# Reciprocal roots by GpSimd's power, and a router's logits and largest eight computed batch by batch in the attention ahead of it

## The chip, the cores and the metric

The kernel runs on one core of a Trainium2 chip. The core has five engines with an instruction stream each: TensorE (PE, with its weight loads PEld), VectorE (DVE), ScalarE (ACT), GpSimd (POOL) and SyncE (SP), which here only issues DMAs. They work side by side and wait for each other through semaphores. The metric is the device time of one execution in microseconds (us); the value compared is the median over runs.

## The reference

A decoder of four layers works on x, 8 sequences of 256 tokens of 256 numbers (2048 tokens). Each layer has three parts, and each part is followed by a residual sum and a layer norm:

```python
def _layernorm(x, axis=-1, eps=1e-05):
    m = jnp.mean(x, axis=axis, keepdims=True)
    v = jnp.var(x, axis=axis, keepdims=True)
    return (x - m) / jnp.sqrt(v + eps)
...
x = _layernorm(x + _L1_xattn_ref(x, ctx_768, ...), axis=-1)
x = _layernorm(x + _L1_ffn_ref(x, ...), axis=-1)
```

The parts that the change touches are five attentions (l0_attn, l0_xattn, l1_attn, l1_xattn, l2_attn; an "xattn" attends to a context of 120 tokens), l3_ffn, a feed-forward in fixed point, and l1_ffn, a mixture of 32 experts of which each token takes 4:

```python
logits = x @ gate_w.T                        # 2048 x 32
probs = jax.nn.softmax(logits, axis=-1)
topk_w, topk_idx = jax.lax.top_k(probs, K)   # K = 4
topk_w = topk_w / jnp.sum(topk_w, axis=-1, keepdims=True)
e_flat = topk_idx.reshape(-1)
order = jnp.argsort(e_flat)
...
pos = jnp.arange(t * K) - starts[e_s]
slot = jnp.minimum(pos, C)                   # C = 256 places per expert
buf = jnp.zeros((E, C + 1, h), x.dtype).at[e_s, slot].set(x[t_s])
```

After it comes l2_xattn, which quantizes its weights to -1, 0 and 1 by the mean of their absolute values, one mean for each of seven matrices:

```python
w_scale = jnp.maximum(jnp.mean(jnp.abs(W)), 1e-05)
qW = jnp.sign(W) * (jnp.abs(W) > 0.5 * w_scale).astype(W.dtype)
```

## The kernel before

The whole state stays on the chip: `X` holds the 2048 tokens as 16 tiles of 128 tokens (tokens on the 128 partitions), `xT` the same transposed. A layer part is a method (`l0_attn`, `l1_xattn`, `l1_ffn`, ...), called in order by `build` (L1881); the weights of the next part are loaded, on SP's queue, into the other of two alternating weight tiles before a part begins. There is no order written out by hand: each engine's instructions are laid out by a scheduler from the program's order and the free buffers, and each engine then works through its own list strictly in order.

**The norm.** `finish_x` (L165) takes z, two tiles of 128x256. `norm_stats` (L141) computes mean and variance on DVE (L146, L147), and `rsqrt` (L126) turns the variance into 1/sqrt(v + eps) with DVE alone: an addition (L129), a first guess by integer arithmetic on the bits (L131), and three Newton steps of three instructions each (L134, L135, L137), all of them on tiles of 128x2. Then X = (z - mean) * rs_y (L170). `transpose_into_xT` (L150) transposes X on PE, and ACT copies it into `xT` (L157). There are 104 such calls of `rsqrt`, one for two tiles of 128 tokens each.

**The attentions of sixteen heads.** `attention16` (L571) runs l1_attn, l1_xattn and l2_attn over eight batches, software-pipelined: while the exponentials of batch b are made (`exps16`), the minima of batch b+1 (`low`, L445 and L461, in `largest16`) are reduced by DVE and the output projection of batch b-1 is done. `sums16` (L538) multiplies the exponentials with the values, divides (`sides` on ACT and DVE, L533 and L534, then `aT` on POOL, L536), adds the bias to X on POOL (`biased`, L558), projects, adds (z, L566) and finishes the norm. l0_attn has a loop of its own with the same end (`biased` L267, z L273). l0_xattn (L320) is a plain loop over batches: scores `psc`, their maximum `nm` (L352), exponential, transposition, product, z (L363), norm.

**The routing in l1_ffn** (L971). Once the norm of l1_xattn is complete, PE computes the logits of all 16 tiles (`plog`), and ACT copies them (L742). `route` (L737) takes the largest eight of each tile with their indices (L746, L747), makes one-hots `oh` in float32 (L753), their sum over the four choices `m` (L761), running sums over tiles `before` (L765), and with two matmuls per tile the position of each token in each expert's queue (`pos`). L1001 to L1009 turn positions into slots with a sentinel for full experts; `pick` (L774) selects each token's own slot with the one-hots (L779, L781); `place` (L1014) is the position inside the expert. `takers` (L797) inverts the map: for each tile and choice it compares `place` with the numbers 0 to 255 (`at`, L818, 64 of them) and multiplies this one-hot with `own`, which holds the token's numbers (L809, L810), so that `take` (L827) says which token stands in which place of which expert. X has been written to memory as `xd` on ACT's queue (L792). Each expert then gathers its 256 rows with two indirect DMAs of POOL (L834), transposes them (L849), multiplies with its weights `we` (loaded on SP's queue through three buffers) and writes its rows `y` to memory (`yd`). A shared expert (`ph` from `sgu`, `silu` L968, `shT` L969) is computed for all tokens ahead of the 32.

**The weights of l2_xattn** are prepared in the time of the experts: `ternary` (L1524) sums absolute values of the seven matrices on DVE (`w_sums`, L1534, from `l2x_flat`, 128 x 7680 numbers), POOL adds over the partitions (`w_scale`, L1538), and DVE compares (L1551, L1553). They lie in the tile of the next-but-one part, loaded while l1_xattn runs.

**l3_ffn** (`fixed_point`, L1438) works on 256 tokens at a time: two matmuls with large DVE passes over 128x2048 between them, z (L1481), norm. The last eight norms write the result.

Of the kernel before, what the change touches and what calls it, by code (L numbers as in the profile page):

```python
# [11 lines left out]
F32 = mybir.dt.float32  # L12
BF16 = mybir.dt.bfloat16
I32 = mybir.dt.int32
U32 = mybir.dt.uint32
AF = mybir.ActivationFunctionType
# [4 lines left out]
P = 128  # L21
# [21 lines left out]
class Net:  # L43
    def __init__(self, ctx: ExitStack, tc: tile.TileContext, ins, out):
# [41 lines left out]
        self.avg = self.const.tile([P, 2, B], F32, name="avg")  # L86
        self.w_scale = self.const.tile([P, len(L2X)], F32, name="w_scale")
        self.wset = 0

# [9 lines left out]

    def load(self, *specs, rows=(), flat=None):  # L100

        self.wset ^= 1
        srcs = [self.ins[name] for name, _ in specs]
        brow = [LAYOUT.rows[name] for name in rows]
        total = sum(src.shape[1] for src in srcs) + sum(n for _, n in brow)
        whole = self.wpool.tile([P, total], F32, name=f"w{self.wset}")
        out, o = [], 0
        for (name, kc), src in zip(specs, srcs):
            part = whole[:, o : o + src.shape[1]]
            self.nc.sync.dma_start(part, src)  # L110
            out.append(part.rearrange("p (c n) -> p c n", c=kc))
            o += src.shape[1]
        for at, n in brow:
            self.nc.sync.dma_start(whole[0:1, o : o + n], self.ins["rows"][:, at : at + n])
            out.append(whole[0:1, o : o + n])
            o += n
        return (out, whole) if flat else out

# [6 lines left out]

    def rsqrt(self, var, n):  # L126
        nc, tmp = self.nc, self.tmp
        v = tmp.tile([P, n], F32, name="rs_v")
        nc.vector.tensor_scalar(v, var, LN_EPS, None, ALU.add)  # L129
# [407 lines left out]

    def sums16(self, b, e, vps, sizes, wo, bo, work):  # L538

# [28 lines left out]

        return project_out, lambda: self.transpose_into_xT(2 * b, 1)

    def attention16(self, project, low, vps, sizes, causal, wo, bo, work):  # L571

# [15 lines left out]
        for b in range(B):  # L588
# [14 lines left out]
            values = vps[b // 2 % 2]  # L603
            before = self.sums16(b, e, [values[:, b % 2, t, :] for t in range(len(sizes))], sizes, wo, bo, work)
            if b % 2 == 0 and b + 2 < B:
# [34 lines left out]
    def load_l1_xattn(self):  # L640
        return self.load(*((f"l1x_w{n}", 2) for n in "qkvo"), rows=("l1x_bv", "l1x_bo"))

    def l1_xattn(self, w):
        nc = self.nc
        wq, wk, wv, wo, bv, bo = w
        with ExitStack() as ctx:
# [14 lines left out]

            self.attention16(project, low, vps, [SC], False, wo, bo, work)

# [301 lines left out]
    def silu_mul(self, out, pg, pu, shape, work):  # L965
# [3 lines left out]
        nc.vector.tensor_tensor(out, g, pu, ALU.mult)  # L969

    def l1_ffn(self, w):  # L971
        nc, tc = self.nc, self.tc
        gate = self.gate1
        E, K, C = 32, 4, 256
        DROP = E * C
        with (
# [10 lines left out]
            slot = keep.tile([P, NT, K], U32, name="slot")  # L987
            with tc.tile_pool(name="f1q", bufs=1) as pool:
                with tc.tile_pool(name="f1r", bufs=1, space=PSUM) as ps:
                    plog = ps.tile([P, NT, E], F32, name="plog")  # L990
                    for i in range(NT):
                        self.mm(plog[:, i, :], [(self.xT4[:, c, i, :], gate[:, c, :]) for c in range(2)])
                    m8, fi, oh, pos, _ = self.route(plog, E, K, pool, ps)
                    nc.vector.tensor_tensor(gw, m8[:, :, :K], m8[:, :, 0:1].to_broadcast([P, NT, K]), ALU.subtract)
                    nc.scalar.activation(gw, gw, AF.Exp)
                    total = pool.tile([P, NT], F32, name="total")
                    nc.vector.tensor_reduce(total, gw, AX.X, ALU.add)
                    nc.vector.reciprocal(total, total)
                    nc.vector.tensor_tensor(gw, gw, total.unsqueeze(2).to_broadcast([P, NT, K]), ALU.mult)
                    first = pool.tile([P, E], F32, name="first")  # L1000
                    nc.vector.tensor_scalar(first, self.cst("iota")[:, :E], float(C), None, ALU.mult)  # L1001
                    full = pool.tile([P, NT, E], F32, name="full")
                    nc.vector.tensor_single_scalar(full, pos, float(C), ALU.is_ge)
                    slotf = pool.tile([P, NT, E], F32, name="slotf")
                    nc.vector.tensor_tensor(slotf, pos, first.unsqueeze(1).to_broadcast([P, NT, E]), ALU.add)
                    left = pool.tile([P, NT, E], F32, name="left")
                    nc.vector.tensor_scalar(left, slotf, -1.0, float(DROP), ALU.mult, ALU.add)
                    nc.vector.tensor_tensor(left, left, full, ALU.mult)
                    nc.vector.tensor_tensor(slotf, slotf, left, ALU.add)  # L1009
                xd = self.in_dram(pool, dram)  # L1010
                slot4 = self.pick(oh, slotf, K, E, pool, "slot4")
                nc.vector.tensor_copy(slot, slot4)
                place = pool.tile([P, NT, K], F32, name="place")
                nc.vector.scalar_tensor_tensor(place, fi, -float(C), slot4, ALU.mult, ALU.add)  # L1014
                with tc.tile_pool(name="f1t", bufs=1, space=PSUM) as ps:
                    take = self.takers(place, oh, K, pool, work, ps, keep)
            pool = ctx.enter_context(tc.tile_pool(name="f1l", bufs=1))
# [133 lines left out]
    def l2_ffn(self, w):  # L1151
# [3 lines left out]
        with ExitStack() as ctx:  # L1155
# [23 lines left out]
            for _ in later:  # L1179
                pass  # L1180
            self.fixed_point(w4, pool, work, ps)

# [341 lines left out]
    def ternary(self, pool):  # L1524
# [4 lines left out]
        for name, k, n, count in L2X:  # L1529
            where[name] = (o, k // P, n, count)  # L1530
            o += k // P * n
        sums = pool.tile([P, len(L2X)], F32, name="w_sums")
        for j, (name, (o, kc, n, _)) in enumerate(where.items()):
            nc.vector.tensor_reduce(  # L1534
                sums[:, j : j + 1], w[:, o : o + kc * n], AX.X, ALU.add, apply_absolute_value=True
            )
        scale = self.w_scale
        nc.gpsimd.partition_all_reduce(scale, sums, P, bass_isa.ReduceOp.add)  # L1538
        for j, (_, _, _, count) in enumerate(where.values()):
# [338 lines left out]
LAYERS = [f"l{n}_{part}" for n in range(3) for part in ("attn", "xattn", "ffn")]  # L1878


def build(tc, ins, out, layers=LAYERS, tap=None):  # L1881
    with ExitStack() as ctx:
        net = Net(ctx, tc, ins, out)
        net.last = tap is None
        net.start()
        w = None
        for n, name in enumerate(layers):
            if w is None:
                w = getattr(net, f"load_{name}")()
            nxt = None  # L1890
            if n + 1 < len(layers):
                nxt = getattr(net, f"load_{layers[n + 1]}")()
            getattr(net, name)(w)
            w = nxt
        if tap:
            tap(net)
# [19 lines left out]
```

## Time and profile before

| | us |
|---|---|
| median of 3 runs | 2713.8 (2710.76 to 2717.37) |
| the profiled execution | 2858.3 |
| its span, first to last instruction | 2856.3 |
| mean granted clock of TensorE in it | 0.867 |

The profile is of a single execution, which took 144.5 us longer than the median; durations in the text below come from that execution. The stages, by their windows in it (us from the start of the span; busy us in the window):

| stage | window | PE | DVE | ACT | POOL | granted clock |
|---|---|---|---|---|---|---|
| l0_attn, last part | 170-216 | 46.0 | 32.8 | 4.4 | 8.3 | 0.74 |
| l0_xattn | 220-310 | 63.8 | 40.6 | 17.4 | 0.0 | 0.71 |
| l1_attn | 680-860 | 160.3 | 122.6 | 64.5 | 23.4 | 0.96 |
| l1_xattn | 860-1010 | 120.6 | 120.3 | 54.3 | 21.0 | 0.90 |
| l1_ffn, routing | 1013-1068 | 30.3 | 43.9 | 1.6 | 0.3 | 0.53 |
| l2_attn | 1250-1540 | 204.7 | 196.5 | 90.7 | 72.5 | 0.86 |
| l3_ffn | 2680-2856 | 140.2 | 148.8 | 61.9 | 0.0 | 0.90 |

What is not in the table: l0_ffn, with 8 experts (about 312 to 680), the 32 experts themselves (1092 to 1226), l2_xattn (1540 to 1700), and a long stretch in which l2_ffn, l3_attn and l3_xattn are interleaved (1700 to 2680).

How to read the lines in the prediction: a line of the timeline gives the start in us, the duration in us, the engine, the line of the kernel, the operation, output and inputs by the program's names, shape, how many instructions are merged in it, and in brackets how long the engine had been idle before it and what released it. A line of the costliest groups gives the count, then busy us and mean ns of one instruction, then the idle time of the engine before them and what ended it. A granted clock below 1 means that TensorE was held below full speed in that stretch.

### The profile page before, as it was taken

To read this page: it belongs to the slowest core of one execution; us is meant where nothing else is said; L and a number is where in the kernel's file an instruction comes from. 1 tells how busy PE (TensorE), PEld (TensorE's weight loads), DVE (VectorE), ACT (ScalarE), POOL (GpSimd) and SP (SyncE) were. 2 spreads that over 40 slices of the span, in tenths; PEclk is the share of its full clock that TensorE was granted. 3 is DMA by queue.
4 is the path that set the end of the run, shared out by engine and by line. 5 is a ranking of instruction groups with operands and counts; after the bars stand their busy time and mean duration, and the time that the engine had idled before them with its cause. 6 is when DMAs were issued, how large, how long until landed. Compare 5 with 4: busy or idle time off the path is not lost.

```text
span 2856.3 us, 41312 instructions
## 1 busy us (share of the span) xinstructions
PE 2197.9 (77%) x14323; PEld 1590.8 (56%) x14332; DVE 1778.5 (62%) x6270; ACT 929.6 (33%) x2125; POOL 843.6 (30%) x850
## 2 busy tenths in 40 slices
PE   8967587869988858835886667678787787777887
PEld 5544476735555547723554345456576675555665
DVE  4674400066667877445777887476586685755778
ACT  2321132323333302202442153235344344343442
POOL 1010021131111103454010015665656655663000
PEclk9988598989998959967998887789899898888899
DMA  2001266610001015731001011111111111120000
GB/s 79 2 1 37 100 244 238 249 36 1 1 15 53 16 45 153 214 102 45 1 1 56 1 45 34 47 43 40 48 38 45 47 39 38 50 74 19 1 12 19
DMA packets 84175, 166.31 MB, mean 58 GB/s; under 512 B 31654, under 2 KB 51254, under 8 KB 80256
## 3 DMA queue, kind: packets, MB, share of 16 engines
q0 software_dynamic: 52288, 110.52, 12.8%
q1 hardware_dynamic: 26746, 47.35, 5.0%
q10 hardware_dynamic: 4934, 5.82, 0.6%
q8 instruction: 114, 1.87, 0.3%
q14 instruction: 93, 0.76, 0.1%
HBM read 242.90 MB, written 17.70 MB: 91 GB/s over the span
## 4 chain that ended last, share of the span: by engine, by line
PE 24%; DVE 16%; issue 6%; another core or an unknown queue 3%; ACT 2%; POOL 1%; DMA 0%; POOLq 0%; DVEq 0%; ACTq 0%
PE po L1266 5%; PE pp L122 4%; PE s L122 4%; PE po L122 2%; DVE low L461 1%; PE s L1412 1%; PE po L1247 1%; PE s L1390 1%; PE sc L122 1%; DVE junk L1214 1%; POOL rows L834 1%; DVE low L445 1%; PE sc L428 1%; DVE X L170 1%
## 5 line engine op out<-in xcount | busy, mean ns | idle before, releaser
L834 POOL DMA_INDIRECT rows<-in_l2f_table_dram,index x512 | 530.0, 1035 | 364.2 <-issue 107.0
L1266 PE MATMUL po<-rows,diag 128*128 128x256 f32 x768 | 233.3, 441 | 95.4 <-ACT diag L1265 68.1
L1214 DVE SCALAR_TENSOR_TENSOR junk<-rows,X 128x256 f32<-128x256 f32 x512 | 214.9, 420 | 52.5 <-DMA rows<-in_l2f_table_dram,index 25.8
L1266 PEld LDWEIGHTS po<-rows,diag 128*128 128x128 f32 x768 | 156.9, 218 | 147.3 <-ACT diag L1265 80.5
L122 PE MATMUL pp<-xT,w 128*128 128x256 f32 (+1 forms) x672 | 195.6, 432 | 39.6 <-issue 25.3
L122 PE MATMUL ph<-xeT,we 128*128 128x128 f32 x1248 | 188.5, 296 | 41.1 <-DMA we<-in_l0f_experts_dram,wrow 35.9
L122 PEld LDWEIGHTS ph<-xeT,we 128*128 128x128 f32 x1248 | 175.0, 206 | 63.8 <-DMA we<-in_l0f_experts_dram,wrow 39.3
L536 POOL TENSOR_TENSOR aT<-sides,inv 128x256 f32<-128x256 f32 x64 | 46.8, 731 | 518.6 <-DVE sides L534 294.2
L122 PEld LDWEIGHTS pp<-xT,w 128*128 128x128 f32 x672 | 139.9, 215 | 74.4 <-issue 34.4
L156 PE MATMUL pt<-ident,X 128*128 128x128 f32 x352 | 78.1, 337 | 128.5 <-DVE X L170 86.8
L1265 ACT ACTIVATE diag<-ident,dots 128x128 f32<-128x128 f32 x384 | 134.7, 394 | 128.9 <-PE po L1266 57.4
L157 ACT COPY xT<-pt 128x512 f32<-128x512 f32 x88 | 51.6, 586 | 369.4 <-PE pt L156 252.7
L834 POOL DMA_INDIRECT xe<-xd,take x87 | 84.4, 970 | 254.6 <-DVE y L946 101.0
L946 DVE TENSOR_TENSOR y<-py,we 128x256 f32<-128x256 f32 x23 | 9.8, 425 | 226.4 <-PE py L122 226.4
L156 PEld LDWEIGHTS pt<-ident,X 128*128 128x128 f32 x352 | 50.7, 167 | 162.8 <-issue 87.8
L122 PE MATMUL py<-we,hT 128*128 128x256 f32 x496 | 131.6, 390 | 0.9 <-DVE hT L969 0.9
L940 ACT ACTIVATE hT<-ph,we 128x128 f32<-128x128 f32 x184 | 65.8, 367 | 148.4 <-PE ph L122 133.5
L500 ACT ACTIVATE e<-sc 128x512 f32<-128x512 f32 (+1 forms) x148 | 78.6, 602 | 103.1 <-PE sc L428 87.7
L428 PE MATMUL sc<-kv,qv 32*128 32x128 f32 (+2 forms) x1496 | 102.7, 320 | 4.9 <-DVE sides L534 1.8
L428 PEld LDWEIGHTS sc<-kv,qv 32*128 32x128 f32 x1496 | 78.9, 191 | 40.8 <-issue 32.9
L428 PE MATMUL sc<-qv,kv 32*128 32x128 f32 (+2 forms) x1368 | 99.6, 346 | 0.1
L122 PE MATMUL sc<-xT,w 128*128 128x512 f32 x204 | 98.2, 629 | 1.1 <-ACT xT L157 0.7
(458 smaller groups left out, 5170.2 us busy)
## 6 DMA issues: line engine op xcount, KB each, us to landing
we<-in_l1f_experts_dram SPq DMA_DIRECT2D x32, 384.0 KB
yd<-y SPq DMA_DIRECT2D x32, 256.0 KB
rows<-in_l2f_table_dram,index POOLq DMA_INDIRECT x512
xd<-X ACTq DMA_DIRECT2D x16, 256.0 KB
w<-in_l2x_w_dram SPq DMA_DIRECT2D x1, 4096.0 KB
yd<-y SPq DMA_DIRECT2D x23, 128.0 KB
X<-in_x_dram SPq DMA_DIRECT2D x8, 256.0 KB
w<-in_l3f_w_dram SPq DMA_DIRECT2D x2, 1024.0 KB
```

The source lines that it names most:

```text
L122: self.nc.tensor.matmul(out, lhsT=lhsT, rhs=rhs, start=n == 0, stop=n == last and bias is None)
L156: nc.tensor.transpose(pt[:, c, j, :], self.X[:, i0 + j * step, c * P : (c + 1) * P], self.ident)
L157: nc.scalar.copy(self.xT4[:, :, i0 : i0 + step + 1 : step, :], pt)
L170: nc.vector.tensor_scalar(self.X[:, i, :], z[:, j, :], mv[:, j, 0:1], r[:, j : j + 1], ALU.subtract, ALU.mult)
L428: nc.tensor.matmul(sc[: shape[0], part], lhsT=lhsT, rhs=rhs, start=mask is None, stop=True, skip_group_check=True)
L500: lambda r, sc: nc.scalar.activation(e0[m][:n0, r], sc, AF.Exp),
L536: nc.gpsimd.tensor_tensor(out, split(both), split(inv), ALU.mult)
L834: self.nc.gpsimd.indirect_dma_start(out=out, out_offset=None, in_=table, in_offset=bass.IndirectOffsetOnAxis(ap=index, axis=0), **({} if r ...
L940: nc.scalar.activation(hT[:, g + f, :], ph[:, f, :], AF.Gelu, bias=b1[:, g + f : g + f + 1])
L1214: nc.vector.scalar_tensor_tensor(junk, row, 1.0, self.X[:, i, :], ALU.mult, ALU.mult, accum_out=out)
L1265: nc.scalar.activation(diag, self.ident, AF.Copy, scale=dots[:, k : k + 1])
L1266: nc.tensor.matmul(po, lhsT=diag, rhs=rows[:, k, D:], start=False, stop=g + k == H * K - 2)
```

## The change

1. `rsqrt` gets a second form, used where `power` is set: in five attentions, and in l3_ffn (48 of the 104 calls). GpSimd adds eps and raises to the power of -0.5; DVE does nothing.
2. l1_xattn calls `choose(b)` after each batch's transposition: it writes X of this batch to memory on SP's queue, computes this batch's logits, and takes the largest eight. They are kept in spare columns of l1_xattn's weight tile.
3. The sums of absolute values of l2_xattn's weights are made at the end of l1_xattn by ACT, with its accumulated output; the reduction over partitions stands at the head of l1_ffn.
4. `route1` takes the place of `route`, `pick` and `takers` in l1_ffn (l0_ffn keeps these): one-hots in bfloat16, their sum by two additions, `own` shared between DVE and ACT, `place` by a product and two additions of halves ahead of a short reduction, a quarter of the `at` on ACT with two activations each, and slots and weights computed from `place` at the end of the program's text.

```diff
+        self.half = self.const.tile([P, 2], F32, name="half")
+        nc.gpsimd.memset(self.half, -0.5)
...
     def rsqrt(self, var, n):
         nc, tmp = self.nc, self.tmp
+        if self.power:
+            v = tmp.tile([P, n], F32, name="rs_v")
+            nc.gpsimd.tensor_scalar(v, var, LN_EPS, None, ALU.add)
+            y = tmp.tile([P, n], F32, name="rs_y")
+            nc.gpsimd.tensor_tensor(y, v, self.half[:, :n], ALU.pow)
+            return y
...
+            def choose(b):
+
+                xd = self.xd1[1 + b * S : 1 + (b + 1) * S, :].rearrange("(t p) d -> p t d", p=P)
+                nc.sync.dma_start(xd, self.X[:, 2 * b : 2 * b + 2, :])
+                pl = self.bank([P, 2, 256])[:, :, :32]
+                for j in range(2):
+                    i = 2 * b + j
+                    self.mm(pl[:, j, :], [(self.xT4[:, c, i, :], self.gate1[:, c, :]) for c in range(2)])
+                lg = work.tile([P, 2, 32], F32, name="lg")
+                nc.scalar.copy(lg, pl)
+                for j in range(2):
+                    i = 2 * b + j
+                    nc.vector.max(self.top1[:, i, :], lg[:, j, :])
+                    nc.vector.max_index(self.top1_i[:, i, :], self.top1[:, i, :], lg[:, j, :])
+
+            self.attention16(project, low, vps, [SC], False, wo, bo, work, then=choose)
...
+                    size = work.tile([P, 2048], F32, name="size", tag="e0")
+                    total = self.w_sums[:, j : j + 1] if not a else work.tile([P, 1], F32, name="more")
+                    nc.scalar.activation(size[:, :m], self.l2x_flat[:, o + a : o + a + m], AF.Abs, accum_out=total)
...
+    def route1(self, E, K, C, gw, slot, pool, work, ps, keep):
...
+        oh = pool.tile([P, K, NT, E], BF16, name="oh")
...
+            nc.vector.tensor_tensor(m2, oh[:, :2], oh[:, 2:], ALU.add)
+            nc.vector.tensor_tensor(m, m2[:, 0], m2[:, 1], ALU.add)
...
+        for i in range(NT):
+            nc.scalar.mul(own[:, :, 1, i, :], oh[:, :, i, :], float(i))
+        nc.vector.tensor_scalar(own[:, :, 0], oh, self.cst("token")[:, 0:1], None, ALU.mult)
...
+        nc.scalar.copy(pos_bf, pos)
+        at_own = pool.tile([P, K, NT, E], BF16, name="at_own")
+        nc.vector.tensor_tensor(at_own, oh, pos_bf.unsqueeze(1).to_broadcast([P, K, NT, E]), ALU.mult)
+        part = at_own.rearrange("p k t e -> p (k t) e")
+        for n in (E // 2, E // 4):
+            half = pool.tile([P, K * NT, n], BF16, name=f"half{n}")
+            with nc.allow_low_precision(reason="one of them is not zero"):
+                nc.vector.tensor_tensor(half, part[:, :, :n], part[:, :, n:], ALU.add)
+            part = half
+        place = pool.tile([P, K, NT], F32, name="place")
+        nc.vector.tensor_reduce(place.rearrange("p k t -> p (k t)"), part, AX.X, ALU.add)
...
+                at = work.tile([P, C], BF16, name="at", bufs=4)
+                if k < K - 1:
+                    nc.vector.tensor_scalar(at, iota, place[:, k, i : i + 1], None, ALU.is_equal)
+                else:
+                    off = work.tile([P, C], BF16, name="off")
+                    nc.scalar.activation(off, iota, AF.Abs, bias=away[:, i : i + 1])
+                    nc.scalar.activation(at, off, AF.Relu, scale=-1.0, bias=self.one)
...
-            nc.vector.tensor_reduce(
-                sums[:, j : j + 1], w[:, o : o + kc * n], AX.X, ALU.add, apply_absolute_value=True
-            )
...
+            self.power = True
             self.fixed_point(w4, pool, work, ps)
...
+POWER = ("l0_attn", "l0_xattn", "l1_attn", "l1_xattn", "l2_attn")
```

## The prediction

> **What bounds the kernel now.** I read the page first: busy shares, then the chain of work that ended last.
>
> ```profile
> span 2856.3 us, 41312 instructions
> PE 2197.9 (77%) x14323; PEld 1590.8 (56%) x14332; DVE 1778.5 (62%) x6270; ACT 929.6 (33%) x2125; POOL 843.6 (30%) x850
> ...
> PE 24%; DVE 16%; issue 6%; another core or an unknown queue 3%; ACT 2%; POOL 1%; DMA 0%; POOLq 0%; DVEq 0%; ACTq 0%
> ```
>
> The named shares of the chain make 52%, led by PE and then DVE, and 77% and 62% are averages over stages with different limits. So each stage the change touches needs its own window (busy us of PE / DVE / POOL): tail of l0_attn 170–216: 28 / 33 / 8; l0_xattn 220–310: 64 / 41 / 0; l1_attn 680–860: 160 / 123 / 23; l1_xattn 860–1010: 121 / 120 / 21; routing 1013–1068: 30 / 44 / 0.3; l2_attn 1250–1540: 205 / 197 / 73; l3_ffn 2680–2856: 140 / 149 / 0. l1_attn is PE's; l0_attn's tail, routing and l3_ffn are DVE's; the rest are chains in which the engines take turns. POOL, which gets the new work, is at most a quarter busy in all of them.
>
> The timeline of one norm (start, duration, engine, line, operation) shows what the first edit takes away:
>
> ```profile
> 1000.21 0.17 DVE L129 TENSOR_SCALAR rs_v<-ln_mv 128x2 f32<-128x2 f32 x1
> 1000.42 0.17 DVE L131 TENSOR_SCALAR rs_y<-rs_v 128x2 int32<-128x2 int32 x1
> ...
> 1002.38 0.74 DVE L170 TENSOR_SCALAR X<-z,ln_mv,rs_y 128x256 f32<-128x256 f32 x2
> 1002.85 0.87 PE L156 MATMUL pt<-ident,X 128*128 128x128 f32 x4 [0.90 <-DVE X L170]
> ```
>
> From rs_v to X 2.17 us pass for eleven operations on two numbers per partition, 0.20 us apart: dependent, so nothing overlaps.
>
> **Powers (48 of 104 norms: 8 each in five attentions and l3_ffn).** DVE loses eleven instructions per norm; POOL gains an add and a power, both 128x2; X waits for POOL. Known terms of the round trip: DVE to POOL 0.17 us (sides end 1006.87, aT starts 1007.04), a further hop back about 0.1, and the fixed part of a POOL operation. That comes from two rows of POOL's groups:
>
> ```profile
> L536 POOL TENSOR_TENSOR aT<-sides,inv 128x256 f32<-128x256 f32 x64 | 46.8, 731 | 518.6 <-DVE sides L534 294.2 <-DVE inv L529 201.9 <-PE sc L428 22.5
> L267 POOL TENSOR_TENSOR biased<-X,bo 128x512 f32<-128x512 f32 x8 | 10.1, 1268 | 39.7 <-DVE z L273 19.8 <-ACT bo L402 12.8 <-DVE rs_a L135 7.0
> ```
>
> (1268−731)/256 = 2.10 ns per element and 194 ns fixed: the add takes 0.2 us. No row shows a power. Below it cannot be under the add, 0.2 us; above, if its work per element were a hundred times a multiply's, 2 × 210 ns + 0.19 = 0.6 us; a thousand times would be 4.4 us. I take 0.5 us, near the hundredfold, because the fixed part dominates two elements. POOL also shows 0.30 us of "issue" between successive operations. Round trip 0.17 + 0.2 + 0.3 + 0.5 + 0.1 = **1.25 us**, gain about 0.9 us where DVE stands still for it, more where DVE has other work in between. The even point is a power of about 1.4 us.
>
> A rule of the Trainium skill speaks against this: GPSIMD Engine Reference, its introduction and section 4.1, call GpSimd the wrong choice for ordinary elementwise arithmetic, about twice as slow as VectorE. In the trace it is right for wide tiles: aT's 731 ns stands beside 0.42 us for a 128x256 X. But two elements cost the fixed parts, 0.16 to 0.20 us on either engine, and here eleven steps become two. By the rule alone, two for one, the norm would cost 2 × 2 × 0.2 = 0.8 us plus two hops: still less than 2.17. What it leaves open is the power's own price.
>
> What is queued behind the wait: in both attention loops X stands right after the variance in DVE's order, so DVE idles the round trip, and the next batch's minima (low, L445 and L461), for which PE's masked scores wait, stand behind X. On POOL one `biased` (1.27 us) of the next batch is queued ahead of some powers. By stage:
>
> - l0_attn's tail: DVE 33 of 46 us, batches 4.4 to 5.6 us apart. Eleven operations go, and so do their collisions with POOL's `biased`:
>
> ```profile
> 174.99 1.27 POOL L267 TENSOR_TENSOR biased<-X,bo 128x512 f32<-128x512 f32 x1 [0.17 <-POOL biased L267]
> ...
> 175.24 1.05 DVE L129 TENSOR_SCALAR rs_v<-ln_mv 128x2 f32<-128x2 f32 x1
> ```
>
> (an operation of 0.17 us takes 1.05 while POOL runs `biased`). 8 × 1.1 = −9.
> - l0_xattn: a serial loop of 9.2 us a batch (z at 267.09, 276.32, 285.21), PE waiting 2.67 us for X. The maxima nm (L352) stand between variance and X, so the round trip is partly covered: after nm, 261.31, X could start instead of at 263.19. 8 × 1.6 = −13.
> - l1_attn: PE busy 89%, so half of 0.9: 8 × 0.45 = −4.
> - l2_attn: about 31 us a batch; X and low follow at once (1400.92 rs_v, 1403.33 X, 1403.97 low, PE's masks waiting 0.80 us for low). 8 × 1.0 = −8.
> - l3_ffn: DVE 149 of 176 us; removed operations lie among large ones, 1.3 to 2.2 us each norm, and other large work covers POOL except in the last norm (2850.23 to 2852.40). 7 × 1.2 + 0.9 = −9.
>
> **Choosing inside l1_xattn.** Each batch gains four logits matmuls on PE (plog's 56 took 9.53 us, so 0.7; at most 1.2), a copy on ACT (0.4), two MAX8 and two FIND_INDEX8 on DVE (0.75), and moves its write of X from ACT's queue (0.37 us of issue) to SP's. SP issues in order: `sgu`, `sd` and the experts' first three loads now stand behind X writes that wait for norms, and the next attention's weights, which reuse the tile that holds the eight largest, stand ahead of the later experts' loads and wait until routing has read it. All of that is over before take, when SP has nothing due; I cost it at nothing, and at up to 3 us if `sgu` lands late. PE and DVE are both at 80%, so I charge 0.7 + 0.3 = 1.0 of the 1.45, against the norm's 0.9: 8 × 0.1 = +1. The eight Abs sums (by the 128x512 exponent at 0.60 us and the 2048-wide Gelu at 1.95, some 3 × 0.65 + 2 × 0.45 + 3 × 2.0 = 8.9 us on ACT) take the hole in which ACT waits for the last projection, 1008.1 to the xT copy at 1023.86. Two of them come before the last `sides` and delay it by 1.3. Sum **+2**.
>
> **Routing.** From z (ends 1013.23) to take (starts 1067.84): 54.6 us, all on the path, since gathers and experts wait for take.
>
> ```profile
> 1013.38 9.53 PE L122 MATMUL plog<-gate,xT 128*128 128x32 f32 x56 [0.88 <-DVE z L566]
> 1022.73 1.09 PE L156 MATMUL pt<-ident,X 128*128 128x128 f32 x4
> 1024.50 1.92 PE L122 MATMUL plog<-gate,xT 128*128 128x32 f32 x8 [0.68 <-ACT xT L157]
> ...
> 1034.17 3.61 DVE L761 TENSOR_REDUCE m<-oh 128x512 bf16<-128x2048 f32 x1
> ...
> 1047.44 2.50 DVE L779 TENSOR_TENSOR pick_t<-oh,slotf 128x512 f32<-128x512 f32 x4
> 1049.97 2.29 DVE L781 TENSOR_REDUCE slot<-pick_t 128x64 f32<-128x2048 f32 x1
> ```
>
> X's transposes stand behind 56 logits matmuls although X was ready at 1017.2, and sixteen MAX8/FIND_INDEX8 follow until 1031.3. z to indices: 18.1 us before. After: norm 2.1 + X 0.7 + transposes 1.0 + copy 0.7 + logits 0.8 + copy 0.5 + two choices 0.9 = 6.7, so −11. Then m by two bfloat16 adds, estimated 1.0 for 3.61 (−2.6); own's second half goes to ACT beside DVE, the first becomes one operation (own took 4 × 0.48 + 4 × 0.69 = 4.7 of DVE; −2 after the part beside other work); the eight operations from full to place, 8.3 us (1044.20 to 1052.5), become a copy of pos on ACT 0.6, a product over 2048, two half sums and a short reduce, estimated 0.6 + 1.2 + 0.6 + 0.4 + 0.6 = 3.4 (−4.9). The 64 `at` took 14.5 us at 0.227 on DVE. Now 48 are DVE's, 10.9 us, and 16 are two activations each on ACT. For that a rule again speaks against: ScalarE: Activation LUTs, rules for kernel authors, says to use VectorE for relu and the like, DVE up to 3 times faster in bfloat16. The nearest row is silu 128x256 at 0.38: 32 × 0.40 = 12.8 us beside DVE's 10.9, a gain of 1.7; by the rule, ACT 3 × 0.227 per activation, 21.8 us, a loss of 7. I take 0.43 per activation, 13.8: −0.7. Routing **−21**.
>
> After take, DVE spent 9.0 us on w_sums (L1534, 1068.43 to 1078.06) with shT queued behind and PE's shared projections waiting on shT's banks; these go to ACT. A POOL wait of 5.8 us before w_scale's reduce also moves ahead of take, where POOL is idle. Projections of 19.5 us then run nearly unbroken instead of 24.4 (1068.12 to 1092.55): **−4**.
>
> **Sum, in the profiled time:** −9 −13 −4 −8 −9 +2 −21 −4 = −66 us of 2858.3 (span 2856.3 and 2.0 around it). That execution is 5% longer than the median, 2713.8, with a granted clock of 0.867; nearly all the gain is DVE's and POOL's fixed time, which I carry over whole, less a tenth for chains that find another wait: −60, **2654 us**.
>
> **Rivals.**
> 1. The power lies near the even point (1.2 to 1.8 us): DVE only trades work for waiting. Norms give −5 where DVE does other work, and routing and experts −23 with l1_xattn at +7 (choosing no longer paid by its norm): about −20, 2694. For it: no row of a power; against: two elements.
> 2. Slower. The power is computed at several us per instruction. Its place is the X that stands directly after the variance: at 4.4 us the round trip is 5.2, +3 per norm, of which some 44 are not covered: +130, less 25, near 2815; it decides from about 2 us, where 44 × 0.6 eats routing's gain. For it: POOL has by far the longest durations per element; against: the hundredfold bound above.
> 3. l1_xattn pays for the choice in full: 1.45 + SP's write and ACT's Abs, 8 × 1.5, and `at` on ACT costs 7: +20 on the sum, 2674. For it: both engines at 80%; against: PE has gaps behind X.
>
> **Numbers.** Forecast 0.62, rival 1 0.12, rival 2 0.10, rival 3 0.16. Lower end: −66 with no tenth lost, a power of 0.2 (40 × 0.3 = 12 more), l0's sixteen norms at their full 2 us (10 more), routing's estimates a third too high (8 more): −96, 2618. Upper end 2700 takes in rivals 1 and 3. A difference under 0.2% (5.4 us) can't be told from none: faster 0.87, same 0.03, slower 0.10.
>
> **What would show it.** rs_y on POOL near 0.5 us and rs_v to X near 1.25 in the attention loops; z to take near 34 us; no w_sums on DVE; l0_xattn's batches 7.6 us apart; low's wait on PE shorter. The forecast is wrong if rs_y exceeds 1.4 us, if l1_xattn's batches exceed 18.7 us by over 1, or if `at` takes over 17 us.

## The result, and the profile after

The changed kernel takes 2678.65 us (median of 4 runs, 2675.02 to 2681.63) against 2715.59 us before. The ratio is 0.9866, with a 95% interval of 0.9847 to 0.9885: 37 us less. The forecast was 60 us less.

The head of the page after, to be read against the one before:

```profile
span 2673.2 us, 40915 instructions
PE 2156.6 (81%) x14331; PEld 1560.5 (58%) x14331; DVE 1678.8 (63%) x5710; ACT 957.6 (36%) x2197; POOL 890.1 (33%) x949
...
PE 20%; DVE 17%; DMA 6%; issue 5%; POOL 2%; ACT 2%; POOLq 0%; ACTq 0%; DVEq 0%
```

DVE lost 100 us of work (1778.5 to 1678.8), and the time fell by little more than a third of that. POOL's new rows, and the row that waits for them, come from the groups of POOL and from the page:

```profile
L143 POOL TENSOR_TENSOR rs_y<-rs_v,half 128x2 f32<-128x2 f32 x48 | 34.1, 712 | 14.4 <-DVE rs_y L154 10.5
L141 POOL TENSOR_SCALAR rs_v<-ln_mv 128x2 f32<-128x2 f32 x48 | 12.4, 259 | 389.2 <-DVE ln_mv L164 358.5
L187 DVE TENSOR_SCALAR X<-z,ln_mv,rs_y 128x256 f32<-128x256 f32 x192 | 72.0, 418 | 52.2 <-POOL rs_y L143 52.1
```

A power of two numbers per partition costs 0.71 us, an addition 0.26 on average (0.22 in the median). DVE now stands 52.1 us in all before X, some 1.1 us at each norm. One norm of l1_xattn in the timeline of the changed kernel, the last one, stands where eleven DVE operations stood:

```profile
990.49 0.30 DVE L164 BATCH_NORM_AGGREGATE ln_mv<-ln_st 128x2 f32<-128x6 f32 x2
...
990.87 0.22 POOL L141 TENSOR_SCALAR rs_v<-ln_mv 128x2 f32<-128x2 f32 x1 [1.51 <-DVE ln_mv L164]
991.17 0.71 POOL L143 TENSOR_TENSOR rs_y<-rs_v,half 128x2 f32<-128x2 f32 x1
991.91 0.73 DVE L187 TENSOR_SCALAR X<-z,ln_mv,rs_y 128x256 f32<-128x256 f32 x2 [1.13 <-POOL rs_y L143]
```

The round trip is 1.12 us, from the variance's end at 990.79 to X at 991.91. The profile shown before is of an execution of 2858 us, and e5 to e8 below ran where the kernel before takes 2851.17 us; so the kernel before was profiled once more (e1), in an execution whose span is 2712.1 us, with which the parts are compared, and of e5 to e8 only ratios and single parts are read. Each part is measured from the start of the last X of the part before it to the start of its own last X, so that the column adds up. (l3_ffn's first passes run beside the last norms of l3_xattn; its row starts at the last X ahead of its first DVE pass.)

| part | before (e1) | after | difference | forecast |
|---|---|---|---|---|
| l0_attn | 213.9 | 207.7 | -6.2 | -9 |
| l0_xattn | 101.1 | 89.0 | -12.1 | -13 |
| l0_ffn | 302.4 | 296.9 | -5.5 | 0 |
| l1_attn | 235.3 | 225.9 | -9.4 | -4 |
| l1_xattn | 159.8 | 172.7 | **+12.9** | +2 |
| l1_ffn: routing, experts | 301.0 | 272.5 | -28.5 | -25 |
| l2_attn | 215.4 | 203.2 | -12.2 | -8 |
| l2_xattn | 163.4 | 168.0 | +4.6 | 0 |
| l2_ffn, l3_attn, l3_xattn | 817.8 | 816.5 | -1.3 | 0 |
| l3_ffn | 198.4 | 214.8 | **+16.4** | -9 |

The sum, unrounded, is -41.2 us; the spans differ by 38.9. The 2.3 us between lie behind the last X: from it to the end of the span 3.9 us pass before and 6.2 in the changed kernel (l3_ffn's power, see the last section). Between profiles of kernels with the same code in a part, a part differs by up to some 5 us (l1_xattn of the changed kernel takes 172.7 us here and 167.7 in e9), so smaller differences are not read one by one. Two parts became longer by more than that, by 29 us together. Those two are what the experiments look into.

### The profile page after: what moved, and what is told of

It is laid out like the page before. It is cut to its first block, busy times and chain, and to the rows that moved or that the text cites. A ratio compares the mean times of both kernels' runs of the same rounds, so it can differ in the third digit from the quotient of the medians.

```text
span 2673.2 us, 40915 instructions
## 1 busy us (share of the span) xinstructions
PE 2156.6 (81%) x14331; PEld 1560.5 (58%) x14331; DVE 1678.8 (63%) x5710; ACT 957.6 (36%) x2197; POOL 890.1 (33%) x949
## 4 chain that ended last, share of the span: by engine, by line
PE 20%; DVE 17%; DMA 6%; issue 5%; POOL 2%; ACT 2%; POOLq 0%; ACTq 0%; DVEq 0%
DMA rows<-in_l2f_table_dram,index 6%; PE s L132 3%; PE pp L132 3%; PE po L1392 3%; PE po L132 3%; DVE junk L1340 2%; DVE low L478 1%; POOL rows L893 1%; PE ph L132 1%; PE sc L132 1%; PE s L1538 1%; PE sc L445 1%; PE s L1516 1%; DVE X L187 1%; DVE top_i L1216 1%
## 5 line engine op out<-in xcount | busy, mean ns | idle before, releaser
L1392 PE MATMUL po<-rows,diag 128*128 128x256 f32 x768 | 218.5, 423 | 43.6 <-ACT diag L1391 41.6
L1392 PEld LDWEIGHTS po<-rows,diag 128*128 128x128 f32 x768 | 149.0, 207 | 91.3 <-ACT diag L1391 65.0
L132 PE MATMUL pp<-xT,w 128*128 128x256 f32 (+1 forms) x672 | 183.4, 411 | 9.6 <-DVE hT L1028 3.3
L132 PEld LDWEIGHTS pp<-xT,w 128*128 128x128 f32 x672 | 131.9, 203 | 40.2 <-issue 9.4
L174 ACT COPY xT<-pt 128x512 f32<-128x512 f32 x88 | 51.5, 586 | 277.0 <-PE pt L173 276.7
L141 POOL TENSOR_SCALAR rs_v<-ln_mv 128x2 f32<-128x2 f32 x48 | 12.4, 259 | 389.2 <-DVE ln_mv L164 358.5
L173 PEld LDWEIGHTS pt<-ident,X 128*128 128x128 f32 x352 | 50.2, 165 | 156.7 <-issue 73.3
L187 DVE TENSOR_SCALAR X<-z,ln_mv,rs_y 128x256 f32<-128x256 f32 x192 | 72.0, 418 | 52.2 <-POOL rs_y L143 52.1
```

Of the source, the lines that this page charges most:

```text
L132: self.nc.tensor.matmul(out, lhsT=lhsT, rhs=rhs, start=n == 0, stop=n == last and bias is None)
L173: nc.tensor.transpose(pt[:, c, j, :], self.X[:, i0 + j * step, c * P : (c + 1) * P], self.ident)
L174: nc.scalar.copy(self.xT4[:, :, i0 : i0 + step + 1 : step, :], pt)
L187: nc.vector.tensor_scalar(self.X[:, i, :], z[:, j, :], mv[:, j, 0:1], r[:, j : j + 1], ALU.subtract, ALU.mult)
L1392: nc.tensor.matmul(po, lhsT=diag, rhs=rows[:, k, D:], start=False, stop=g + k == H * K - 2)
```

## The experiments

No kernel below leaves out work.

**e1: the kernel before, again.**

> The kernel before, unchanged, profiled once more, since its profile on record was of an execution 5% longer than its median. Theory A (the record's profile was slow in the interleaved stretch 1704 to 2654, whose code is the same): ratio 1.000, a profiled execution near 2715 us in which that stretch takes some 815 us as in the changed kernel, and the parts up to the end of l2_attn still about 70 us longer than in the changed kernel; then some 35 us must be given back after it. Theory B (the record's profile was slow everywhere): the parts up to the end of l2_attn take about 37 us more than in the changed kernel, and nothing is given back later.

Measured: 2713.94 us, ratio 1.0003 [0.9987, 1.0019]. Theory A: the stretch of l2_ffn, l3_attn and l3_xattn, with its 512 gathers by POOL, took 949.3 us in the profile shown first, 817.8 us here, and 816.5 in the changed kernel. Of the other parts l1_ffn differs by 8 us between the two profiles of the kernel before (308.9 and 301.0), every other one by less than 4; why the stretch takes longer in some executions was not looked into. Up to the end of l2_attn the changed kernel is 61 us ahead (1528.9 to 1467.9; some 70 were expected), and 22 us of that are given back.

**e2: the power alone.** The edit is `rsqrt`'s second form, with `POWER` and the line ahead of `fixed_point`, put into the kernel before.

> The kernel before with the power form of the root alone, in the same 48 norms. The round trip from variance to X in the changed kernel's trace is about 1.45 us against 2.4 before. Theory A (each norm on a chain gives about 0.9 us, and the sixteen of l0 more): 30 to 40 us less, ratio 0.985 to 0.989, that is nearly the whole change. Theory B (the norms only trade work for waiting, the routing gives the gain): 0 to 10 us less, ratio 0.996 to 1.000.

Measured: 2685.42 us, ratio 0.9889 [0.9852, 0.9926], 30 us less (20 to 40 by the interval). Theory A: the roots carry most of the gain. By parts: l0_attn -8.3, l0_xattn -15.4, l1_attn -9.7, l1_xattn -12.8, l2_attn -8.8, 55 us together, but l3_ffn +16.4.

**e3: the changed kernel without the power.**

```diff
-POWER = ("l0_attn", "l0_xattn", "l1_attn", "l1_xattn", "l2_attn")
+POWER = ()
...
-            self.power = True
             self.fixed_point(w4, pool, work, ps)
```

> The changed kernel with no power form anywhere, roots on DVE as before; choosing in l1_xattn, the sums on ACT and the new routing stay. Theory A: the routing gives about 28 us and its successor stages a few, l1_xattn takes back some 15 to 20: 10 to 20 us less than before, ratio 0.993 to 0.996. Theory B: nearly the whole gain stays, ratio 0.986 to 0.989.

Measured: 2710.33 us, ratio 0.9990 [0.9977, 1.0002]. Neither theory: less is left than A had. l1_ffn gained 26.6 us, and l1_xattn lost 22.1 (181.9 against 159.8). Without the power, parts 2 to 4 of the change nearly cancel each other.

**e4: roots on DVE in l3_ffn alone.** Only the second edit of e3's diff.

> The changed kernel, but the last eight norms (l3_ffn) on DVE as before. Prediction's step: those norms give 9 us, so this is 9 us slower than the changed kernel, ratio to before 0.990. Rival: l3_ffn's norms stand among large DVE operations that now wait for POOL, so they give nothing or lose (l3_ffn took 221 us against 203 in the two profiles): ratio 0.986 or less.

Measured: 2660.82 us, ratio 0.9808 [0.9780, 0.9835]: 18 us *faster* than the changed kernel. The rival. l3_ffn takes 198.4 us. The timeline of PE shows what differs: first the changed kernel, then e4. `ph` is a pass's first product, `po` its second. Each fence begins in the `po` of the fourth of eight passes, goes on to that of the fifth, and shows where the `ph` of the sixth stand.

```profile
2575.12 3.72 PE L132 MATMUL po<-w,v 128*128 128x256 f32 x16
2578.77 0.69 PE L134 MATMUL po<-b,ones 1*128 1x256 f32 x2
2579.45 1.56 PE L132 MATMUL ph<-xT,w 128*128 128x256 f32 x6
2580.85 3.62 PE L132 MATMUL po<-w,v 128*128 128x256 f32 x16
...
2589.30 9.35 PE L132 MATMUL ph<-xT,w 128*128 128x256 f32 x42
```

```profile
2577.72 3.72 PE L132 MATMUL po<-w,v 128*128 128x256 f32 x16
2581.37 0.69 PE L134 MATMUL po<-b,ones 1*128 1x256 f32 x2
2582.06 5.45 PE L132 MATMUL ph<-xT,w 128*128 128x256 f32 x24
2587.34 3.62 PE L132 MATMUL po<-w,v 128*128 128x256 f32 x16
```

A pass has 32 `ph` instructions, and 8 of the sixth pass's stand further ahead in both kernels. In e4 the other 24 stand between the `po` of the fourth and of the fifth pass, so DVE has the sixth pass to work on when the fifth ends. In the changed kernel only six do; the last 18 follow after both, at 2589.30, with those of later passes. DVE there finishes two norms and then waits for the sixth pass, as its timeline shows:

```profile
2592.09 0.74 DVE L187 TENSOR_SCALAR X<-z,ln_mv,rs_y 128x256 f32<-128x256 f32 x2 [1.13 <-POOL rs_y L143]
2593.99 1.23 DVE L1587 TENSOR_SCALAR v<-v 128x2048 f32<-128x2048 f32 x1 [1.16 <-ACT v L1585]
```

From the end of the fourth pass's statistics at 2582.3 to 2594.0 DVE stands idle 7.1 us in five waits. The same pattern comes again two passes later, so that from the first DVE pass over `v` of the fourth pass to that of the eighth 88.6 us go by, against 71.4 in e4: this is the whole loss. No line of l3_ffn's products was edited. The scheduler laid out PE's list otherwise once the roots had left DVE. e8 tests whether that order is the cause.

**e5 and e6: what choosing costs in l1_xattn's loop.** Both start from e4. e5 leaves the logits in the loop and ties the choices behind the last X; e6 leaves only the write of X in the loop.

```diff
 # e5
-                lg = work.tile([P, 2, 32], F32, name="lg")
-                nc.scalar.copy(lg, pl)
-                for j in range(2):
...
+                nc.scalar.copy(lgs[:, 2 * b : 2 * b + 2, :], pl)
...
+            with self.tc.issue_after(self.last_x.ins):
+                for i in range(NT):
+                    nc.vector.max(self.top1[:, i, :], lgs[:, i, :])
+                    nc.vector.max_index(self.top1_i[:, i, :], self.top1[:, i, :], lgs[:, i, :])
 # e6
                 nc.sync.dma_start(xd, self.X[:, 2 * b : 2 * b + 2, :])
+
+            def choose_late(b):
                 pl = self.bank([P, 2, 256])[:, :, :32]
...
+            for b in range(B):
+                choose_late(b)
```

> Of the kernel of e4 (2660.8 us; l1_xattn 171.5 us there from norm to norm, 159.8 before and 146.9 with the power alone): the logits stay in l1_xattn's loop, but all sixteen MAX8 and FIND_INDEX8 stand behind the last X on DVE. Theory D (DVE, in order, stands at each MAX8 until PE's logits and ACT's copy are there, 2.6 us in one batch, with the divisions queued behind it): l1_xattn 10 or more us shorter, 4 to 5 us of choices added at its end, together 2651 to 2656 us. Theory P (PE pays: eight logits matmuls of 0.24 us per batch, 15 us over the loop, stand in PE's order): l1_xattn at most 4 us shorter, together 2660 to 2665.

> Of the kernel of e4: only the write of X stays in the loop; logits, copies and choices of all batches stand behind it. Theory D and theory P alike: l1_xattn goes back to about 148 us, logits and choices add about 13 behind it: 2648 to 2652 us. If the loop's loss lies in what stays (the writes on SP's queue, the sums on ACT), l1_xattn keeps 165 or more and the time is 2665 to 2675.

Measured: e5 ratio 0.9784 [0.9755, 0.9813], e6 0.9751 [0.9719, 0.9783]. By parts, from the profiles:

| | l1_xattn | last X to take | both |
|---|---|---|---|
| before (e1) | 159.8 | 51.5 | 211.3 |
| power alone (e2) | 147.0 | 54.5 | 201.5 |
| changed kernel | 172.7 | 33.6 | 206.3 |
| changed kernel again (e9) | 167.7 | 33.6 | 201.3 |
| e4 | 171.5 | 33.3 | 204.8 |
| e5, choices late | 161.4 | 34.1 | 195.5 |
| e6, logits late too | 151.2 | 37.8 | 189.0 |

Theories D and P both have a share, about half each: the choices cost the loop 10.1 us and the logits 10.2. (Six profiles with the choices in this loop and the power in its norms, among them e7, e8 and e12, lie between 167.7 and 172.7 us, so each share is known to a few us.) The change's own place for them lost about as much on the loop as it saved behind it: with the power alone, and the old routing, the two stretches take 201.5 us, and in those six profiles 201.3 to 206.4. In e6 the work put behind the loop costs only 4.5 us there (forecast 13), because PE does 22 of those matmuls around the last norm, where it would wait for X. A batch in the loop of the changed kernel, in time order:

```profile
941.51 1.92 PE L566 MATMUL pt<-e,vp 120*32 120x256 f32 x10
941.62 0.59 ACT L174 COPY xT<-pt 128x512 f32<-128x512 f32 x1 [1.85 <-PE pt L173]
943.36 1.92 PE L132 MATMUL sc<-gate,xT 128*128 128x32 f32 x8
945.21 1.06 PE L566 MATMUL sc<-e,vp 120*32 120x256 f32 x2
945.31 0.21 ACT L701 COPY lg<-sc 128x64 f32<-128x64 f32 x1 [3.11 <-PE sc L132]
945.56 0.29 DVE L704 MAX8 w<-lg 128x8 f32<-128x32 f32 x2 [2.60 <-ACT lg L701]
...
946.20 0.90 PE L497 MATMUL sc<-ident,low 128*128 128x128 f32 x3
...
947.14 1.41 DVE L499 SCALAR_TENSOR_TENSOR qv<-sc,consts,qv 128x512 f32<-128x512 f32 x2 [0.93 <-PE sc L497]
```

The logits stand in the middle of the sums of the same batch on PE: xT was ready at 942.2, the logits begin at 943.36 and end at 945.28. MAX8, in DVE's order, waits 2.60 us for them with nothing else done on DVE. This is the longest of the loop's seven such places in this profile; their waits add up to 9.6 us.

**e7: the sums of absolute values on DVE again.** From e4, `ternary`'s loop of reductions and its reduction over partitions are as before the change, and ACT's loop at the end of l1_xattn goes.

> Of the kernel of e4: the sums of absolute values and their reduction over partitions are again where the kernel before has them, on DVE after take, nothing else. Prediction's step: the move gave 4 us behind take and cost 1.3 at the last batch, so 2663 to 2664 us here. Rival: the sums on ACT hold up more than the last batch, so the time falls below 2658; or the nine us on DVE were hidden behind the gathers, and nothing changes (2659 to 2662).

Measured: ratio 0.9815 [0.9783, 0.9846]. Its parts decide more sharply than the ratio: l1_xattn 172.7 us (e4 171.5), so ACT's sums cost that loop nothing that shows; from take to the first expert's product on DVE (hT) 25.4 us against 20.4 in e4 (27.2 before). Moving the sums gave 5 us of these, against the 4 us of the forecast.

**e8: another written order in l3_ffn, with the power.**

```diff
-        for o in range(0, NTOK, T):
+        def ahead(o):
             v = work.tile([P, FC, T], F32, name="v")
...
+            return v
+
+        nxt = ahead(0)
+        for o in range(0, NTOK, T):
+            v = nxt
             v = v.rearrange("p f t -> p (f t)")
...
+            if o + T < NTOK:
+                nxt = ahead(o + T)
             h = v.rearrange("p (f t) -> p f t", t=T)
```

> The changed kernel (2678.7 us, l3_ffn 214.8 us, power in it) with one edit in l3_ffn: the first matmuls of the next pass are written ahead of the second matmuls of this pass, so that PE's order has them so, as it has in the kernel with DVE's roots. Theory O (the loss of 16 us in l3_ffn is PE's order, which came out differently once the roots left DVE): l3_ffn at most 198 us, 2655 to 2662 us together. Theory W (the loss is DVE standing 1.13 us for POOL in front of X and what that delays): l3_ffn stays at 210 or more, 2674 to 2679.

Measured: ratio 0.9762 [0.9732, 0.9792]; l3_ffn takes 194.8 us, where the changed kernel takes 214.8. Theory O. Its PE timeline has the sixth pass's `ph` between the two `po` again:

```profile
2714.72 3.72 PE L132 MATMUL po<-w,v 128*128 128x256 f32 x16
2718.37 0.69 PE L134 MATMUL po<-b,ones 1*128 1x256 f32 x2
2719.07 6.31 PE L132 MATMUL ph<-xT,w 128*128 128x256 f32 x28
2725.22 3.62 PE L132 MATMUL po<-w,v 128*128 128x256 f32 x16
```

**e12: the same order, roots of l3_ffn on DVE.** The edit of e8 in the kernel of e4.

> The kernel of e4 (roots of l3_ffn on DVE) with l3_ffn's passes in e8's written order. Tells how much of e8's 195 us in l3_ffn is the power's and how much the order's: if the power is worth the prediction's 9 us under one and the same order, l3_ffn takes 204 here; if it is worth nothing, 195; 198 as in e4 means 3 us for the power.

Measured: 2658.92 us, ratio 0.9773 [0.9743, 0.9802]; l3_ffn 195.1 us. Under one written order the power is worth nothing in l3_ffn (195.1 without it, 194.8 with it in e8 and e10), though DVE works 8 us less there (156.7 us busy against 164.7): what was taken away did not stand on the path. With the end of the span taken in, where the power costs 2.3 us, it loses 2 us.

**e9, e10, e11: the changed kernel again, both repairs together, and the comparisons.** e10 has the edits of e6 and e8. e11 adds to e10:

```diff
-                if k < K - 1:
+                if k < K:
```

> The changed kernel, unchanged, beside the next three on one chip. All theories: ratio to before 0.9866, the stages as in its first profile (l1_xattn 172.7 us, last X to take 33.6, l3_ffn 214.8).

> The changed kernel with the two edits of e6 and e8: logits and choices behind l1_xattn's loop, and l3_ffn's passes written in the other order, with the power. If the two losses are separate and as read (17 us from l1_xattn to take, 19 us in l3_ffn): 36 us less than the changed kernel, ratio to before about 0.973. If they overlap with something later: less than 25 us.

> The kernel of e10 with all 64 comparisons of the routing on DVE, none on ACT. In the changed kernel ACT's two activations per tile (0.49 and 0.51 us) set the loop at 0.95 us per tile; DVE alone needs 4 x 0.227 = 0.91. Theory: last X to take changes by less than 1 us. Rule that ScalarE is the wrong engine here: it falls by 3 us or more. Opposite: it grows by 3 us because small DVE work of the routing no longer has a hole.

Measured: e9 2680.10 us, ratio 0.9856 [0.9825, 0.9887]; e10 **2640.19 us**, ratio 0.9707 [0.9679, 0.9736]; e11 2641.48 us, 0.9718 [0.9690, 0.9746]. e9's profile has l1_xattn at 167.7 us, 5 less than the first. e10 is 40 us faster than the changed kernel beside it (36 expected) and beats both kernels: the two losses are separate. In e11 the stretch from the last X to take falls from 37.8 to 34.9 us, close to the 3 us that it was to fall if ScalarE is the wrong engine here, and the sum of the kernel shows none of it (1.3 us slower, inside the intervals). In its profile all 64 comparisons are one line, 12.74 us:

```profile
993.47 12.74 DVE L1089 TENSOR_SCALAR at<-iota_bf,place 128x256 bf16<-128x256 bf16 x64
```

In the changed kernel a tile takes 0.95 us of ACT's two activations and the loop 15.6 us, with DVE waiting 0.27 us for PE to free a buffer in most of them. As to where e11's 2.9 us went: its l1_ffn is 2.4 us shorter than e10's and its l2_attn, which no edit touched, 3.1 us longer, a difference that the same part also has between other profiles (203.1 to 207.3 us).

## Why the prediction was right, and which of its sizes were off

**Direction and range** held: faster by 37 us, inside 2618 to 2700. The size was 23 us too large, and the errors of the steps are larger than that, since some have opposite signs: l1_xattn and l3_ffn missed by 36 us together, while l1_attn, l1_ffn, l2_attn and the unedited l0_ffn came out 19 us better than forecast. That the total still lies well inside the range is in part luck.

- *Power.* Round trip forecast 1.25 us, measured 1.12. The power itself was taken at 0.5 and measures 0.71; the "issue" gap of 0.30, which POOL's gathers show, is only 0.08 between these two operations (991.09 to 991.17), which makes up for it. Rival 1 and rival 2 fall with that: 0.71 is half the even point. The rule of the Trainium skill that sends elementwise work to VectorE and not to GpSimd (GPSIMD Engine Reference, section 4.1) would, taken by itself, have kept the roots on DVE; in e2 the five attentions are 55 us shorter with them on POOL.
- *l0_attn, l0_xattn.* -9 and -13 forecast, -6.2 and -12.1 measured (in l0_attn's tail, 170-216, PE was busy 28.2 us, as the prediction has it; the 46.0 in the table of stages is the window's length). l0_xattn's batches came 7.24 us apart (X at 260.23, 267.47), forecast 7.6.
- *l1_attn.* "PE busy 89%, so half of 0.9": -4 forecast, -9.4 measured, and -9.7 in e2. Halving was the error: the gain is 1.2 us per batch, where the round trip is 1.05 us shorter than the chain. PE waits there for the minima (`low`), which stand behind X in DVE's order; these waits fell from 16.7 us (e1) to 11.3, as the prediction's last sign had it. l2_attn, -8 forecast, gave -12.2 and in e2 -8.8; within what this part varies the forecast held.
- *Choosing inside l1_xattn.* **This step failed in size**: +2 forecast, +12.9 measured, and +22.1 without the norms' gain (e3). Two terms were mis-sized. "Plog's 56 took 9.53 us, so 0.7" counted four matmuls per batch, but each of the four is two instructions in the trace, so eight: 1.06 to 1.92 us (1.08 at 905.27, where the granted clock was 1.00; 1.92 at 943.36, where it was 0.50). And of DVE only its own 0.75 us was counted, not its standing still for the logits in its order (2.60 us in that batch, 9.6 over the loop; the choices' place cost 10.1, e5). The 1.3 us charged for ACT's sums do not show (e7). The prediction's sign for this, batches longer by over 1 us, came true: the last seven came 17.2 us apart, X to X, before and 18.8 after. The prediction asked what is queued behind the norm's wait, but not behind this one. Rival 3 had the engines' cost in full and nearly the price (8 x 1.5), though not the wait, and its 2674 lies nearest to the result, by luck in part, since it has nothing of l3_ffn; its other half, `at` on ACT costing 7, was 1.1 (15.6 us, 1009.27 to 1024.91, against 14.5) and 2.9 against DVE alone (e11).
- *Routing.* z to take: 54.6 us before, 35.7 after (989.78 to 1025.5), -18.9 against -21 forecast. The comparisons on ACT account for most of what is missing: 0.50 us an activation where 0.43 was taken. The row to hand (silu, 0.38) and the prediction's estimate from the rule of the Trainium skill (ScalarE: Activation LUTs, rules for kernel authors; 0.68) bracket the 0.50; that rule's factor, "up to about 3×", is per element, and the prediction laid it on the whole instruction. The place chain took 3.8 us from the last matmul of pos (1005.37) to 1009.16, forecast 3.4.
- *After take.* -4 forecast; take to the first hT went from 27.2 to 20.1 us, -7.1, of which e7 gives 5 to the sums.
- *l3_ffn.* **This step failed.** "Removed operations lie among large ones ... other large work covers POOL": -9 forecast, +16.4 measured. That DVE is busy 149 of 176 us was read as each removed operation shortening the stage. e12 shows that they shorten it by nothing under one order, and e8 that the 16 us are the order of PE's list, which the scheduler changed when the roots left DVE. The end of the program, 2.3 us longer with POOL at work in the last norm, is in no term of the sum. The prediction asked of this stage only what DVE and POOL do, the engines that the edit names, and took PE's order as given.

What stays open: l0_ffn (-5.5) and l2_xattn (+4.6) have no edit of their own; the same parts range from 296.9 to 303.7 and from 162.3 to 169.6 us over all profiles here, so nothing is concluded from them. What of l1_xattn is left over the power alone in e6 (151.2 against 147.0) was not split further. e10 with the roots of l3_ffn on DVE, which the 2 us above speak for, was not run.

## What to carry to other kernels

A chain of many tiny dependent operations costs its number of steps, not its elements; handing it to an idle engine in two steps pays when the round trip (here 1.12 us) is shorter than the chain (2.17 us) and the chain is what the next stage waits for, and pays nothing where the engine has other work in that time. When small work is moved into a pipelined loop to shorten a serial stretch, price the wait at its head in the in-order engine, not only its own duration: here the loop lost about as much as the stretch gained, until the work went behind the loop's end, where it filled a hole. And where a scheduler lays out the lists, compare every engine's order in every stage that was touched: an edit on DVE and POOL moved PE's matmuls and cost 16 us.

## What the runs showed of the hardware that was not expected

- GpSimd and VectorE were seen to delay each other in both directions. Before, a DVE addition of 0.17 us took 1.05 beside `biased`; after, two of POOL's 48 additions of 0.22 take 1.16, both while DVE works on 128x2048. One of them, from the timeline of the changed kernel:

```profile
2550.10 1.23 DVE L1589 TENSOR_SCALAR n<-v 128x2048 f32<-128x2048 f32 x1
2550.24 1.16 POOL L141 TENSOR_SCALAR rs_v<-ln_mv 128x2 f32<-128x2 f32 x1 [3.96 <-DVE ln_mv L164]
```

- POOL's work in the very last norm lengthened the end of the program. In the five kernels with the power in l3_ffn the span runs on for 6.2 us after the last X, in the others for 3.9. The longest of POOL's three DRAIN instructions at the end of the changed kernel starts at 2666.2, beside the last power, and takes 6.23 us (each number: shortest, median and longest in ns, first and last start in us), so that it ends 2.3 us after SP has done with its own waits, at 2670.1:

```profile
L2035 POOLq DRAIN  x3: 46/102/6232, 2666.2 to 2673.0; - x3
L2035 SPq DRAIN  x3: 7/7/7, 2670.1 to 2672.7; - x3
```

- The granted clock over l1_xattn was 0.88 before (e1) and 0.90 with the power alone, 0.81 to 0.85 in the six profiles with the choices in the loop, 0.89 in e5 and 0.90 in e6. From e4 (0.82) to e5, with the same 1291 matmul instructions, PE's busy time fell from 142.3 to 129.3 us. So part of the choices' 10.1 us may be the clock's, and so may the 5 us between the two profiles of the changed kernel (0.81 and 0.85). Whether the gaps in PE's work bring the lower clock or the lower clock fills out the gaps was not separated.
